# An attention-and-convolution kernel on one core: every product and transpose issued as two halves of 64 stationary columns

## The chip, the core and the metric

The kernel runs on one core of a Trainium2 chip, as one program with one launch. The metric is the time of one execution on the device in microseconds; the figure for a kernel is the median over its runs. All data is fp32.

## What is computed

Eight images of 768 channels by 32 x 32 pixels go through two residual layers. Cut to what matters, the reference is:

```python
# layer 0: attention whose scores come from variances; _gn is a normalisation over 32 groups of channels
qkv = tokens(_gn(x)) @ W_qkv.T                       # 8 x 1024 tokens x (3 x 768); q is not used
var_v, var_k = var(v, per head), var(k, per head)    # one number per token and head (12 heads of 64)
scores = var_v @ var_k.T * scale                     # an outer product, 1024 x 1024 for each head
out = softmax(scores) @ v @ W_proj.T + b_proj
x = x + out
# layer 1: a 1x1 convolution over 768 features and 28 local correlations
f = _gn(x)
corr = 28 sums over channels of shifted, normalised f * f      # a 7x7 neighbourhood, four lines through it
x = x + conv_w @ concat(f, corr) + conv_b
```

## The kernel before

**Products.** The three large products (keys and values, projection, convolution) are each split into 2 x 2 blocks and computed with seven block products instead of eight. A block product is a *unit*: three accumulating matmuls of 128 rows and 128 stationary columns. In `KeysValues.unit` (L592) the stationary operand is the image and the moving operand 384 columns of weights; in `Wide.unit` (L973, projection and convolution) the stationary operand is a weight block and the moving operand 512 tokens. Both hand their list of operand pairs to `Banks.product` (L342), whose `begin` (L345) issues the matmuls at L359 into one of two x banks and two y banks of PSUM; one early case is issued at L605. When a unit is done, VectorE (or ScalarE, for copies of keys and values) takes the bank.

**Attention.** For each image there are six pairs of heads. `Pair.exponentials` (L716) has ScalarE make the exponentials of one token tile for both heads (two passes of 128 x 1024, L721). `Pair.products` (L740) then multiplies them by the values at L746: four matmuls, each of 64 stationary columns, the two heads on columns 0 to 63 and 64 to 127 of the array. Such a step is issued in runs of four (`Attention.run`, L951, `STEPS = 4`). The row sums of the softmax come either from ScalarE (`denominators`, L725) or from accumulated exponentials, summed by a matmul of 32 stationary columns (`sum_up`, L772, L779) or of 64 (`sum_up_last`, L822, L829).

**The rest on TensorE.** `Corr.gram` (L1070, L1083) multiplies shifted windows of the features in matmuls of 64 stationary columns and 133 moving ones, two sides next to each other. `Wide.join` (L986, L990) adds the correlations' part with matmuls of 64 rows and 128 columns, two of them on the upper and the lower half of the rows; `Conv.corr` (L1253, L1260) does it for the last image. Four small things use the whole array: the group means (`Norm.means` L465, `Norm.spreads` L476, one moving column), and the transposes in `to_rows` (L538), `Pair.spread` (L855) and `Corr.scale.to_dram` (L1139).

**Order.** The schedule is by hand: while the program is built, a `Clock` (L77) carries an estimated time forward, units pass it on by `KV_US`, `T_US`, `STEP_US`, `GRAM_US` and `CORR_US` (L52 to L54), and jobs that are due are issued on the way. `work_off` (L1290) puts attention's runs in as soon as its exponentials should be there, and fills the time between with units of key/value products, convolution and grams. So TensorE changes often between products, runs of attention, grams, joins and transposes. Each engine then executes its instructions in the order so written.

Of the kernel before, what the change touches and what calls it, by code (L numbers as in the profile page):

```python
# [6 lines left out]
F32 = mybir.dt.float32  # L7
# [6 lines left out]
P = 128  # L14
# [3 lines left out]
NH, HD = 12, 64  # L18
HP = NH // 2
MT = N // P  # L20
HF = N // 2
# [11 lines left out]
PAD = 99  # L33
# [6 lines left out]
NROW = NA + 2  # L40

HH = NH // 2
# [6 lines left out]
TBLOCKS = 7  # L49
HELD = 12  # L50
TAIL = 14.0
EXP, SUM, STEP_US = 1.07, 1.15, 1.77  # L52
KV_US, T_US, CORR_US = 1.94, 2.6, 1.05
GRAM_US = 1.45  # L54

# [7 lines left out]
FIRST, LAST = (1, 5, 2), (4, 3, 2)  # L65
# [92 lines left out]
def two_layers(ctx, tc, x, wkv, wproj, bproj, wconv, wcorr, bconv, out):  # L158
    nc = tc.nc
# [4 lines left out]
    const = pool("const", 1)  # L164
# [14 lines left out]
    st = pool("st", 1)  # L179
# [9 lines left out]
    vector = Vector(nc.vector, clock)  # L189
    ready = set()  # L190

    def work(shape, name):
        return wk.tile(shape, F32, tag="wk", name=name)
# [136 lines left out]
            return self.tiles.pop(0)  # L330


    class Banks:
        def __init__(self):
            self.count, self.due, self.open, self.free = {"x": 0, "y": 0}, {}, {}, {}
# [9 lines left out]
        def begin(self, g, p, width, pairs, stop=True, between=None):  # L345
            bank = BANK[p]
            of = "x" if bank == "x" else "y"
            if p in FIRST:
                slot = of, self.count[of] % 2
                self.count[of] += 1  # L350
                self.finish(slot)
                clock.pass_time(max(self.free.get(slot, 0.0) - clock.now, 0.0))
                t = (xbank if of == "x" else ybank).tile([P, width], F32, tag=of, name=f"{bank}{self.count[of]}")
                self.open[g, bank] = slot, t
            slot, t = self.open[g, bank]
            self.finish(slot)
            clock.pass_time(max(self.free.get(slot, 0.0) - clock.now, 0.0))
            for k, (lhsT, rhs) in enumerate(pairs):
                nc.tensor.matmul(  # L359
                    t, lhsT=lhsT, rhs=rhs, start=p in FIRST and k == 0, stop=stop and k == len(pairs) - 1,  # L360
                    skip_group_check=True,
                )
                if between and k == 0:
                    between()
            return slot, t
# [12 lines left out]
    ident = const.tile([P, P], F32, name="ident")  # L378
# [3 lines left out]
    for base, sign in ((0, 1), (3, -1)):  # L382
        nc.gpsimd.affine_select(
            out=group, in_=group, compare_op=ALU.is_ge, fill=0.0, base=base,
            pattern=[[-4 * sign, P // 4], [0, 4]], channel_multiplier=sign,
        )
    group_m = group.rearrange("p g r -> p (g r)")
# [5 lines left out]
    neghalf = const.tile([P, 4], F32, name="neghalf")  # L393
    nc.gpsimd.memset(neghalf, -0.5)

    wcorr_sb = const.tile([P, J, P], F32, name="wcorr_sb")
    nc.gpsimd.memset(wcorr_sb, 0.0)
    cs = const.tile([P, 3, HF], F32, name="cs")
# [7 lines left out]
    rows = [dconst.tile([NROW, ROW], F32, name=f"rows{i}") for i in range(2)]  # L406
# [47 lines left out]
    class Norm:  # L454
# [7 lines left out]
        def means(self):  # L462
            name, mv = self.name, self.mv
            pm = small(f"pm{name}")
            nc.tensor.matmul(pm[:, 0:1], lhsT=group_m, rhs=mv[:, 0:1], start=True, stop=True)  # L465
            self.mean = st.tile([P, 1], F32, tag="mean", bufs=2, name=f"mean{name}")
            vector.tensor_copy(self.mean, pm[:, 0:1])
            d = st.tile([P, 1], F32, tag="d", name=f"d{name}")
            vector.tensor_tensor(d, mv[:, 0:1], self.mean, ALU.subtract)
            self.e = st.tile([P, 1], F32, tag="e", bufs=2, name=f"e{name}")  # L470
            vector.scalar_tensor_tensor(self.e, d, d, mv[:, 1:2], ALU.mult, ALU.add)

        def spreads(self):
            name = self.name
            pv = small(f"pv{name}")
            nc.tensor.matmul(pv[:, 0:1], lhsT=group_m, rhs=self.e, start=True, stop=True)  # L476
            ve = st.tile([P, 1], F32, tag="ve", name=f"ve{name}")
            vector.tensor_scalar(ve, pv[:, 0:1], GN_EPS, None, ALU.add)
            self.rstd = st.tile([P, 1], F32, tag="rstd", bufs=2, name=f"rstd{name}")
            nc.gpsimd.tensor_tensor(self.rstd, ve, neghalf[:, 0:1], ALU.pow)  # L480
# [54 lines left out]
    def to_rows(cols, dr, name):  # L535

        pt = small(f"pt{name}")
        nc.tensor.transpose(pt[0 : MT * HH, 0:P], cols.rearrange("p h t -> p (h t)"), ident)  # L538
        rs = work([MT * HH, P], f"rs{name}")
        vector.tensor_copy(rs, pt[0 : MT * HH, 0:P])  # L540
        nc.sync.dma_start(out=dr.rearrange("h (t p) -> (h t) p", p=P), in_=rs)

    class KeysValues:
# [48 lines left out]
        def unit(self, half, d, n, g, p):  # L592
            b = self.b
            if n == 0:
                self.make_sums(half, (2 * d, 2 * d + 1))
            s = self.sums[g]
            a = {1: self.block(g, 0, 0), 2: self.block(g, 0, 1), 4: self.block(g, 1, 1)}
            a.update({5: s[:, 0], 6: s[:, 1], 7: s[:, 2], 3: s[:, 3]})
            w = kv_stream.tiles[b, half, d, p]
            pairs = [(a[p][:, k, :], w[:, k, :]) for k in range(JH)]  # L600
            taken = lambda ps: self.take(half, g, p, ps)
            if p == 2 and not b + half + d:
                ps = other([P, KW], f"z{g}")
                for k, (lhsT, rhs) in enumerate(pairs):
                    nc.tensor.matmul(ps, lhsT=lhsT, rhs=rhs, start=k == 0, stop=k == len(pairs) - 1)  # L605
                later.after(KV_US + 0.1, lambda: taken(ps))
            else:
                banks.product(g, p, KV_US, KW, pairs, taken)
            if p not in [q for _, q in (PAIR if b + half + d else OPENING)[n + 1 :]]:
                kv_stream.done((b, half, d, p))  # L610
            if d == 1 and n == len(PAIR) - 1:
                self.over = half == 1
                later.after(KV_US + 0.5, lambda: later.after_dve(0.0, lambda: self.spread(half)))
# [77 lines left out]
    class Pair:  # L691
# [153 lines left out]
            invert(0)  # L845

        def invert(self):
            self.inv = st.tile([P, 2 * MT], F32, tag="inv", bufs=2, name=f"inv{self.b}_{self.hp}")
            vector.reciprocal(self.inv, self.sums.rearrange("p e t -> p (e t)"))
            later.after_dve(3.5, self.spread)  # L850

        def spread(self):
            b, hp = self.b, self.hp
            pt = small(f"it{b}_{hp}")
            nc.tensor.transpose(pt[0 : 2 * MT, 0:P], self.inv, ident)  # L855
            row = work([2 * MT, P], f"ir{b}_{hp}")
            vector.tensor_copy(row, pt[0 : 2 * MT, 0:P])
            dr = dpool.tile([2 * MT, P], F32, tag="inv", name=f"di{b}_{hp}")
            nc.sync.dma_start(out=dr, in_=row)
            later.after(4.0, lambda: self.load_inverses([dr[e * MT : e * MT + 1, :] for e in range(2)]))  # L860
# [190 lines left out]
    class Corr:  # L1051
# [18 lines left out]
        def gram(self, t):  # L1070
# [32 lines left out]

            later.after(GRAM_US + 0.25, out)

# [16 lines left out]
        def scale(self, hf, dd):  # L1122

            b = self.b
            m = st.tile([P, 4], F32, tag="m", name=f"m{b}_{hf}")
            vector.tensor_scalar(m, dd[:, :, 0], NORM_EPS2, None, ALU.max)
            rn = st.tile([P, 4], F32, tag="rn", name=f"rn{b}_{hf}")
            nc.gpsimd.tensor_tensor(rn, m, neghalf, ALU.pow)

            def columns():  # L1130
                dn = st.tile([P, 4, NROW], F32, tag="dn", name=f"dn{b}_{hf}")
                vector.tensor_copy(dn[:, :, 0], rn)
                for q in range(4):
                    vector.scalar_tensor_tensor(dn[:, q, 1:NROW], dd[:, q, :], rn[:, q : q + 1], mask, ALU.mult, ALU.mult)
                later.after_dve(0.7 if b else 4.0, lambda: to_dram(dn))

            def to_dram(dn):
                pt = small(f"ct{b}_{hf}")
                nc.tensor.transpose(pt[0 : 4 * NROW, 0:P], dn.rearrange("p q r -> p (q r)"), ident)  # L1139
                cr = work([4 * NROW, P], f"cr{b}_{hf}")  # L1140
                vector.tensor_copy(
                    cr.rearrange("k (y s x) -> k y s x", y=4, s=2),
                    pt[0 : 4 * NROW, 0:P].rearrange("k (s y x) -> k y s x", s=2, y=4),
                )
                for q in range(4):
                    at = PAD + hf * HF + q * P
                    nc.sync.dma_start(out=rows[b % 2][:, at : at + P], in_=cr[q * NROW : (q + 1) * NROW, :])
                if hf == 1:
                    later.after(3.0, self.gather)

            later.after_dve(2.5, columns)
# [273 lines left out]
    for b in range(NB + 1):  # L1425
# [6 lines left out]
        if b:  # L1432
# [3 lines left out]
            f, acc = layer1[b - 1] if b > 1 else first_f * 2  # L1436
# [5 lines left out]
            first, start = (0.0, has_f, conv.sums.first), (0.0, (), conv.start)  # L1442
# [69 lines left out]
```

## Time and profile before

| | before |
|---|---|
| median of 3 runs | 2679.1 us (2678.01 to 2680.77) |
| the profiled execution | 2675.76 us |
| its span, first to last instruction | 2674.0 us |
| granted TensorE clock | 0.998 |
| DVE, ACT, POOL busy | 1604.2, 1364.0, 410.8 us |
| DMA, mean | 167 GB/s |

An fp32 matmul appears in the trace as two records (passes), each with a weight load (PEld) of its own; a transpose appears as one. Durations of single matmul records overlap, since matmuls are pipelined: the distance from the start of one to the start of the next is the time that TensorE gives to it. In a line of the timeline, the columns are the start, the length, the engine, the line of code, the operation, out<-in, stationary rows*columns, and the count of records that were merged.

### The profile page before, as it was taken

To read this page: it belongs to the slowest core of one execution; us is meant where nothing else is said; L and a number is where in the kernel's file an instruction comes from. 1 tells how busy PE (TensorE), PEld (TensorE's weight loads), DVE (VectorE), ACT (ScalarE), POOL (GpSimd) and SP (SyncE) were. 2 spreads that over 40 slices of the span, in tenths; PEclk is the share of its full clock that TensorE was granted. 3 is DMA by queue.
4 is the path that set the end of the run, shared out by engine and by line. 5 is a ranking of instruction groups with operands and counts; after the bars stand their busy time and mean duration, and the time that the engine had idled before them with its cause. 6 is when DMAs were issued, how large, how long until landed. Compare 5 with 4: busy or idle time off the path is not lost.

```text
span 2674.0 us, 30536 instructions
## 1 busy us (share of the span) xinstructions
PE 2634.8 (99%) x9831; PEld 1221.7 (46%) x9831; DVE 1604.2 (60%) x4110; ACT 1364.0 (51%) x1841; POOL 410.8 (15%) x442
## 2 busy tenths in 40 slices
PE   7999999999999999999999999999999999999999
PEld 4443454345543355434554345543455434554344
DVE  5758734775446854478534785348753577536864
ACT  1498069711597116970179701797018960189600
POOL 4220030002310033000330003300133001320000
PEclk9999999999999999999999999999999999999999
DMA  7764455455554555536456265562655626545243
GB/s 285 289 226 156 141 187 150 136 185 165 177 171 133 185 156 179 178 114 208 149 172 195 91 212 157 164 206 73 220 169 159 194 83 226 167 136 165 87 125 101
DMA packets 323354, 446.03 MB, mean 167 GB/s; under 512 B 59458, under 2 KB 245170, under 8 KB 323194
## 3 DMA queue, kind: packets, MB, share of 16 engines
q1 hardware_dynamic: 321962, 441.32, 51.6%
q10 hardware_dynamic: 1232, 2.75, 0.3%
q8 instruction: 79, 1.29, 0.2%
q14 instruction: 81, 0.66, 0.1%
HBM read 377.49 MB, written 64.40 MB: 165 GB/s over the span
## 4 chain that ended last, share of the span: by engine, by line
PE 93%; DMA 4%; DVE 2%; issue 0%; ACT 0%; SPq 0%; POOL 0%; DVEq 0%; POOLq 0%; ACTq 0%
PE x L359 36%; PE av L746 24%; PE y L359 17%; PE z L359 9%; PE gr L1083 3%; DMA x<-x1d 1%; PE den L779 1%; PE x L990 1%; PE y L990 1%; PE z L990 1%; DMA vdr<-rsv 0%; DMA x1d<-f 0%; DVE x L152 0%; DVE v L152 0%; PE den L829 0%
## 5 line engine op out<-in xcount | busy, mean ns | idle before, releaser
L721 ACT ACTIVATE ex<-bc,nk 128x1024 f32<-128x1024 f32 x768 | 826.5, 1137 | 432.2 <-DMA bc<-vdr 171.0
L746 PE MATMUL av<-ex,v 128*64 128x512 f32 x3072 | 691.7, 597 | 5.6 <-ACT ex L721 5.6
L731 ACT ACTIVATE junk<-bk,vm 128x1024 bf16<-128x1024 f32 x368 | 420.3, 1142 | 38.3 <-DMA bk<-kdr 32.4
L746 PEld LDWEIGHTS av<-ex,v 128*64 128x64 f32 x3072 | 223.4, 137 | 434.8 <-issue 372.4
L152 DVE TENSOR_TENSOR acc<-acc,ex 128x1024 f32<-128x1024 f32 x300 | 344.7, 1211 | 0.0
L214 ACT COPY kp<-x 128x384 f32<-128x384 f32 x28 | 13.4, 477 | 571.4 <-PE x L359 571.4
L359 PE MATMUL y<-kv,s 128*128 128x384 f32 x744 | 260.6, 491 | 0.2 <-issue 0.2
L359 PE MATMUL x<-kv,xn 128*128 128x384 f32 x756 | 257.2, 489 | 2.8 <-DVE xn L152 1.6
L359 PE MATMUL x<-kv,s 128*128 128x384 f32 x744 | 254.4, 489 | 0.0
L359 PEld LDWEIGHTS x<-kv,xn 128*128 128x128 f32 x756 | 143.5, 191 | 107.2 <-issue 9.1
L359 PEld LDWEIGHTS x<-kv,s 128*128 128x128 f32 x744 | 138.6, 190 | 102.5 <-issue 9.9
L359 PEld LDWEIGHTS y<-kv,s 128*128 128x128 f32 x744 | 137.8, 190 | 94.2 <-issue 7.3
L480 POOL TENSOR_TENSOR rstda<-vea,neghalf 128x1 f32<-128x1 f32 x8 | 4.8, 595 | 1009.5 <-DVE vea L152 1009.5
L1068 POOL TENSOR_TENSOR turn<-f,ones 128x384 f32<-128x384 f32 x112 | 111.6, 1016 | 265.9 <-PE gr L1083 206.5
L359 PE MATMUL x<-v,wt 128*128 128x512 f32 x288 | 130.2, 596 | 0.0
L359 PE MATMUL z<-kv,xn 128*128 128x384 f32 x372 | 126.9, 488 | 0.0
L152 DVE TENSOR_TENSOR v<-y,v 128x128 f32<-128x128 f32 x180 | 41.0, 282 | 138.7 <-PE y L359 138.7
L359 PE MATMUL x<-f,wt 128*128 128x512 f32 x252 | 116.1, 600 | 0.3 <-DVE x L152 0.3
L584 POOL TENSOR_TENSOR s<-xn 128x384 f32<-128x384 f32 x64 | 66.8, 1054 | 287.1 <-PE x L359 193.3
L152 DVE BATCH_NORM_STATS2 vbn<-v 128x6 f32<-128x64 f32 x720 | 101.6, 209 | 0.0
L152 DVE SCALAR_TENSOR_TENSOR x<-x,bconv_sb,x 128x512 f32<-128x512 f32 x63 | 45.8, 746 | 92.6 <-DMA x<-x1d 52.8
L359 PEld LDWEIGHTS z<-kv,xn 128*128 128x128 f32 x372 | 69.9, 190 | 49.2 <-issue 2.3
(191 smaller groups left out, 3012.9 us busy)
## 6 DMA issues: line engine op xcount, KB each, us to landing
kv<-kvs SPq DMA_DIRECT2D x124, 576.0 KB
kv<-in_wkv_dram SPq DMA_DIRECT2D x95, 576.0 KB
bc<-vdr SPq DMA_DIRECT2D x96, 512.0 KB
f<-in_x_dram SPq DMA_DIRECT2D x48, 512.0 KB
bk<-kdr SPq DMA_DIRECT2D x46, 512.0 KB
x1d<-f SPq DMA_DIRECT2D x42, 512.0 KB
x<-x1d SPq DMA_DIRECT2D x42, 512.0 KB
out_dram<-x SPq DMA_DIRECT2D x82, 256.0 KB
```

The source lines that it names most:

```text
L152: return getattr(self.engine, name)(*args, **kw)
L214: nc.scalar.copy(to, at)
L359: nc.tensor.matmul(t, lhsT=lhsT, rhs=rhs, start=p in FIRST and k == 0, stop=stop and k == len(pairs) - 1, skip_group_check=True,)
L480: nc.gpsimd.tensor_tensor(self.rstd, ve, neghalf[:, 0:1], ALU.pow)
L584: nc.gpsimd.tensor_tensor(self.sums[g][:, 0], a[g][2], a[g][3], ALU.add)
L721: nc.scalar.activation(ex, self.bc[e], AF.Exp, scale=self.kv.nk[self.half][:, h, t : t + 1])
L731: nc.scalar.activation(junk, self.bk[e], AF.Exp, scale=self.kv.m2[self.half][:, h, t : t + 1], accum_out=self.sums[:, e, t : t + 1],)
L746: nc.tensor.matmul(self.av[e * HD : (e + 1) * HD, hf, :], lhsT=self.vt[:, t, e, :], rhs=exs[e][:, hf * HF : (hf + 1) * HF], start=t == 0, ...
L779: nc.tensor.matmul(den[at * 32 : (at + 1) * 32, :], lhsT=ones[:, 0:32], rhs=self.acc[e][:, hf * HF : (hf + 1) * HF], start=True, stop=True,)
L990: nc.tensor.matmul(t, lhsT=wcorr_sb[at, i, :], rhs=cs[at, tokens, :], start=False, stop=True, skip_group_check=True)
L1068: nc.gpsimd.tensor_tensor(to[:, :, side], half, windows(ones, ones.ap[0], (0, J), (HW, 4), (1, HW)), ALU.mult)
L1083: nc.tensor.matmul(ps[side * HD : (side + 1) * HD, :n].rearrange("p (y x) -> p y x", x=WIDE), lhsT=block[:, j, side, :], rhs=image[:, 4 * ...
```

## The change

Every matmul of 128 stationary columns at L359, L605, L465 and L476 becomes two of 64 columns, one after the other, with the same moving operand, into the upper and the lower half of the same PSUM tile. The transposes become plain matmuls of 64 (or 48) columns with the identity as the moving operand, without the transpose flag. The one at L855 had 16 columns; its input is now a constant tile of 64 columns of which 16 are filled. The one at L1139 had 80; it is now two of 64 that overlap by 48 columns, and the rows of the last quarter are read from the second. The matmuls of 32 columns (L779) and of 64 rows (L990, L1260) stay. The planner's estimates change.

```diff
-EXP, SUM, STEP_US = 1.07, 1.15, 1.77
-KV_US, T_US, CORR_US = 1.94, 2.6, 1.05
-GRAM_US = 1.45
+EXP, SUM, STEP_US = 1.07, 1.15, 1.73
+KV_US, T_US, CORR_US = 1.93, 2.58, 1.2
+GRAM_US = 1.4
...
+    def halves(out, lhsT, rhs, start=True, stop=True, **kw):
+
+        for at in (slice(0, HD), slice(HD, P)):
+            nc.tensor.matmul(out[at], lhsT=lhsT[:, at], rhs=rhs, start=start, stop=stop, **kw)
+
+    def turned(out, columns):
+        nc.tensor.matmul(out, lhsT=columns, rhs=ident, start=True, stop=True)
+
...
-                nc.tensor.matmul(
-                    t, lhsT=lhsT, rhs=rhs, start=p in FIRST and k == 0, stop=stop and k == len(pairs) - 1,
-                    skip_group_check=True,
+                halves(
+                    t, lhsT, rhs, start=p in FIRST and k == 0, stop=stop and k == len(pairs) - 1, skip_group_check=True
                 )
...
+    invs = [const.tile([P, HD], F32, name=f"invs{n}") for n in range(2)]
+    for t in invs:
+        nc.gpsimd.memset(t, 1.0)
...
-            nc.tensor.matmul(pm[:, 0:1], lhsT=group_m, rhs=mv[:, 0:1], start=True, stop=True)
+            halves(pm[:, 0:1], group_m, mv[:, 0:1])
...
-            nc.tensor.matmul(pv[:, 0:1], lhsT=group_m, rhs=self.e, start=True, stop=True)
+            halves(pv[:, 0:1], group_m, self.e)
...
-        nc.tensor.transpose(pt[0 : MT * HH, 0:P], cols.rearrange("p h t -> p (h t)"), ident)
+        turned(pt[0 : MT * HH, 0:P], cols.rearrange("p h t -> p (h t)"))
...
-                    nc.tensor.matmul(ps, lhsT=lhsT, rhs=rhs, start=k == 0, stop=k == len(pairs) - 1)
+                    halves(ps, lhsT, rhs, start=k == 0, stop=k == len(pairs) - 1)
...
-            self.inv = st.tile([P, 2 * MT], F32, tag="inv", bufs=2, name=f"inv{self.b}_{self.hp}")
-            vector.reciprocal(self.inv, self.sums.rearrange("p e t -> p (e t)"))
+            self.inv = invs[self.hp % 2]
+            vector.reciprocal(self.inv[:, 0 : 2 * MT], self.sums.rearrange("p e t -> p (e t)"))
...
-            nc.tensor.transpose(pt[0 : 2 * MT, 0:P], self.inv, ident)
+            turned(pt[0:HD, 0:P], self.inv)
...
-                nc.tensor.transpose(pt[0 : 4 * NROW, 0:P], dn.rearrange("p q r -> p (q r)"), ident)
-                cr = work([4 * NROW, P], f"cr{b}_{hf}")
+                columns, over = dn.rearrange("p q r -> p (q r)"), 4 * NROW - HD
+                turned(pt[0:HD, 0:P], columns[:, 0:HD])
+                turned(pt[HD:P, 0:P], columns[:, over:])
+                cr = work([P, P], f"cr{b}_{hf}")
...
-                    at = PAD + hf * HF + q * P
-                    nc.sync.dma_start(out=rows[b % 2][:, at : at + P], in_=cr[q * NROW : (q + 1) * NROW, :])
+                    at, row = PAD + hf * HF + q * P, q * NROW + (HD - over) * (q == 3)
+                    nc.sync.dma_start(out=rows[b % 2][:, at : at + P], in_=cr[row : row + NROW, :])
```

More of the change, by code (lines that the diff above doesn't have):

```diff
@@ L1138, in to_dram @@
                 pt = small(f"ct{b}_{hf}")
-                nc.tensor.transpose(pt[0 : 4 * NROW, 0:P], dn.rearrange("p q r -> p (q r)"), ident)
-                cr = work([4 * NROW, P], f"cr{b}_{hf}")
+                columns, over = dn.rearrange("p q r -> p (q r)"), 4 * NROW - HD
+                turned(pt[0:HD, 0:P], columns[:, 0:HD])
+                turned(pt[HD:P, 0:P], columns[:, over:])
+                cr = work([P, P], f"cr{b}_{hf}")
                 vector.tensor_copy(
                     cr.rearrange("k (y s x) -> k y s x", y=4, s=2),
-                    pt[0 : 4 * NROW, 0:P].rearrange("k (s y x) -> k y s x", s=2, y=4),
+                    pt[:, 0:P].rearrange("k (s y x) -> k y s x", s=2, y=4),
                 )
                 for q in range(4):
-                    at = PAD + hf * HF + q * P
-                    nc.sync.dma_start(out=rows[b % 2][:, at : at + P], in_=cr[q * NROW : (q + 1) * NROW, :])
+                    at, row = PAD + hf * HF + q * P, q * NROW + (HD - over) * (q == 3)
+                    nc.sync.dma_start(out=rows[b % 2][:, at : at + P], in_=cr[row : row + NROW, :])
                 if hf == 1:
```

## The prediction, made before the changed kernel ran

> **What bounds the kernel now.** I read the page's busy times first, then its chain, then the stages, then the timeline of TensorE at the places where it changes from one kind of work to another.
>
> ```profile
> span 2674.0 us, 30536 instructions
> ...
> PE 2634.8 (99%) x9831; PEld 1221.7 (46%) x9831; DVE 1604.2 (60%) x4110; ACT 1364.0 (51%) x1841; POOL 410.8 (15%) x442
> ...
> PE 93%; DMA 4%; DVE 2%; issue 0%; ACT 0%; SPq 0%; POOL 0%; DVEq 0%; POOLq 0%; ACTq 0%
> ```
>
> TensorE is busy all the time and 93% of the chain is its own. But a busy PE isn't a PE at its peak: a matmul that waits inside the array counts as busy. So I take the distance from start to start. The timeline of one stage, with key/value products, a transpose, a gram, products, a transpose:
>
> ```profile
> 1008.32 4.03 PE L359 MATMUL x<-kv,xn 128*128 128x384 f32 x12
> 1012.19 2.10 PE L359 MATMUL y<-kv,s 128*128 128x384 f32 x6
> 1014.12 0.27 PE L538 MATMUL ptv<-ident,vm 128*48 128x128 f32 x1
> 1014.32 1.58 PE L1083 MATMUL gr<-f,turn 128*64 128x133 f32 x24
> 1015.84 2.20 PE L359 MATMUL y<-kv,s 128*128 128x384 f32 x6
> 1017.87 0.27 PE L538 MATMUL ptk<-ident,nk 128*48 128x128 f32 x1
> 1017.98 2.42 PE L359 MATMUL x<-kv,s 128*128 128x384 f32 x7
> ```
>
> Twelve passes of a product take 1012.19 - 1008.32 = 3.87 us, 0.3225 each; six take 1.93, the same, though a transpose follows. From a transpose to a product it is 0.11 (1017.87 to 1017.98), to the gram 0.20: 0.09 lost. The gram's 24 records are 12 pairs 0.113 us apart, 1.36, and take 1.52: 0.15 lost. The six passes after it take 2.03, not 1.935: 0.10 lost. About 0.35 us for going into 64 columns and back. Around attention:
>
> ```profile
> 1082.33 2.10 PE L359 MATMUL x<-kv,s 128*128 128x384 f32 x6
> 1084.35 7.09 PE L746 MATMUL av<-ex,v 128*64 128x512 f32 x32
> 1091.37 2.20 PE L359 MATMUL x<-kv,s 128*128 128x384 f32 x6
> 1093.41 0.27 PE L1139 MATMUL ct<-ident,dn 128*80 128x128 f32 x1
> 1093.52 2.10 PE L359 MATMUL y<-kv,s 128*128 128x384 f32 x6
> ```
>
> 2.02 for six passes (0.09 over), 7.02 for 16 pairs of 0.429 (0.15 over), 2.04 for the next six (0.10 over): 0.35 again. So the two shapes run at the same rate (a pair of 64-column passes over 512 takes 0.429 us, as one pass of 128 columns in the projection does) and the change between them costs.
>
> Over the whole trace, all matmul starts split the time thus: 13.8 us before the first; 2552.1 of passes at their steady distance (moving columns / 1.2 per ns + 2.5 ns, which fits 133, 384 and 512); 58.4 at changes of shape; 44.9 of stalls proper; 4.8 after the last start and in remainders. Of the stalls, 31.2 us lie in the first two images; each image from the third to the seventh has under 2.2. The stages say the same:
>
> ```profile
> 0.00:328.00 328.00, 306.03 (x1035) 145.23 (x1036) 235.66 (x650) 159.22 (x210) 67.71 (x80) 1.00 0.64 222
> 328.00:656.00 328.00, 320.07 (x1182) 149.01 (x1181) 193.06 (x446) 169.08 (x221) 54.11 (x56) 0.99 0.51 164
> 656.00:984.00 328.00, 327.47 (x1229) 151.48 (x1228) 193.83 (x505) 171.71 (x234) 51.06 (x54) 1.00 0.52 165
> ```
>
> (length, then busy PE, PEld, DVE, ACT, POOL, clock, DMA): from the third image PE is idle 0.5 us in 328, at full clock.
>
> [...] 93 to 114 ns lost on leaving a shape, none between the two column halves of attention. [...] the 48-column transposes follow products without loss, so they run in the full shape[...]. [...] the trace's first pass after a change loses 104 and 51 (24 with 32 columns), so it is a load that nothing hides.
>
> **The change, part by part.**
> 1. *Changes of shape.* One costs the drain (medians: 93 ns leaving 128x128, 100 leaving 64 columns, 97 leaving 64 rows, 114 leaving 32 columns) plus the first load. Before there are 338, with the transposes counted as full shape: 58.4 us. In the changed program's order of matmuls 116 remain, at joins and 32-column sums: 45 from 64 columns to 64 rows x (100+104) = 9.2; 37 back x (97+51) = 5.5; 17 from 32 to 64 columns x (114+51) = 2.8; 9 from 64 and 8 from the joins to 32 x 0.12 = 2.1. Sum 19.6. **Saved 38.8.** The direct change from 64 columns to 64 rows isn't in the trace; 93 or 100 as its drain moves the sum by 0.3.
> 2. *Halved products.* 4704 passes become pairs. Attention's and gram's pairs give the steady distance of a whole pass, the second half 7 ns after the first, hidden by the next pair. Loads: gram hides two per 0.113 us, a product has 0.3225. Twice the instructions at 4 per 0.3225 us is below gram's 4 per 0.113. **Nothing**; its cover is that overlap, and without it each ns per pass is 4.7 us. No row has the same moving columns in both halves (attention streams two tiles, gram two overlapping windows of one), so this stays the open point; below nothing it can't go, the pass being bound by its columns.
> 3. *Transposes.* 63, each one pass of 109 ns, become two passes: **+6.9**; 16 have two halves, 3.5 more if those don't run side by side.
> 4. *Group means.* 32. A matmul of one column hides no load: 112 ns to the next product and 84 over in that one's first pass, two loads of 128 columns. Half the columns, half of 168: **-2.7** (0 to -5.4).
> 5. *Waits given back.* In the first two images the waits are for loads and ScalarE, and TensorE saves about 8 us there ((58.4-19.6+2.7-6.9)/8 = 4.3 per image); what comes before a wait that ends at a fixed time is lost. I take **+2** (0 to 8). In later images the fourth step of a run starts about 1.0 us after its exponentials end (their buffer is freed by the run's first step), but 0.2, 0.3 and 0.0 in three runs of the second and third pairs, where ScalarE also sums. An earlier TensorE finds these late: **+1** (0 to 8: three runs x eight images x the 0.35 of one excursion).
> 6. *Order.* With the planner's smaller figures some units move one place ahead of a run of attention; the work and the DMAs are the same but for two memsets on POOL (idle 85%) and a copy of 128 rows in place of 80 on DVE, as long by its columns. Nothing: the moved unit's PSUM and weights are those of its neighbour, and if one is late it is part 5.
>
> Sum: -38.8 + 6.9 - 2.7 + 3 = -31.6. Profiled execution 2675.8 - 31.6 = 2644.2 (span about 2642.4). The median shown is 3.3 above that execution; the same 31.6 off 2679.1 gives **2647.5**. Ends: -38.8 + 6.9 - 5.4 = -37.3, or 2641.8; -38.8 + 6.9 + 3.5 + 16 = -12.4, or 2666.7.
>
> **Rivals.** *The gain is waited away* (ScalarE's exponentials and the early loads take both ends of part 5, +16): -34.6 + 16, **2660.5**. For it: slack of 0.0 to 0.3 us; against: ACT is busy 172 of 328 us per image, and its next exponential starts when TensorE frees a buffer, so it moves along. *The halves don't overlap fully* (at L359, both reading the same columns): with two offsets of 6.7 ns per pass, 4704 x 13.4 ns = +63, giving **2710.5** with parts 1, 3, 4 and 5, slower than before; it decides from 31.6 / 4704 = 6.7 ns per pass. Against: 1366 pairs of attention show no such ns. *The loss isn't the shape's* but any change of work's: nothing saved, +6.9 - 2.7, **2683.3**. Against: products to transposes, and x to y to z bank, cost nothing.
>
> **Numbers.** Forecast 81%, waits 13%, offset 4% (half of it near no change, as one offset just cancels the gain), not the shape 2%. About 0.2% (5 us) is what the measurement can tell from no change. Faster 94%, within 2%, slower 4%. The range, 2638 to 2663, takes in the forecast's lower end with the runs' spread and the first rival; above it lie 2 of the rivals and the far end of the waits.
>
> **What would show it.** Right: a product's six passes before and after attention take 1.935 us (2.02 and 2.04 now), 16 attention pairs 6.87; a pair of a product's halves every 0.3225 or 0.429; 116 changes worth 20 us; images 328 us apart now, then 324. Wrong: pairs at a larger distance, second halves starting late, stalls before attention's fourth steps, or losses where the shape doesn't change.

## The result, and the profile after

| | before | changed |
|---|---|---|
| median | 2679.24 us (2678.01 to 2680.77, 4 runs) | 2657.34 us (2655.61 to 2658.48, 4 runs) |
| ratio | | 0.9917, 95% interval 0.9900 to 0.9935 |
| profiled execution | 2675.76 us, span 2674.0 | 2655.61 us, span 2653.9 |

Faster by 21.9 us, where 31.6 were forecast (2647.5): inside the range, 9.8 us short. The page of the changed kernel, with the lines that answer to those of before:

```profile
span 2653.9 us, 40302 instructions
...
PE 2602.3 (98%) x14694; PEld 1307.0 (49%) x14694; DVE 1605.4 (60%) x4110; ACT 1368.4 (52%) x1841; POOL 414.3 (16%) x444
...
PE 91%; DMA 4%; DVE 2%; ACT 1%; issue 1%; SPq 1%; POOL 0%; DVEq 0%; POOLq 0%; ACTq 0%
```

There are half as many matmul records again, in less time, and the chain has 1% each in ScalarE, SP's queue and issue that it did not have. The same stage as before in TensorE's timeline (products, a transpose, a gram, products, a transpose):

```profile
1010.19 2.10 PE L336 MATMUL y<-kv,s 128*64 128x384 f32 x12
1012.12 0.27 PE L339 MATMUL ptv<-ident,vm 128*48 128x128 f32 x1
1012.13 0.33 PE L1093 MATMUL gr<-f,turn 128*64 128x133 f32 x1
1012.23 0.27 PE L339 MATMUL ptv<-ident,vm 128*48 128x128 f32 x1
1012.29 1.46 PE L1093 MATMUL gr<-f,turn 128*64 128x133 f32 x22
1013.54 0.49 PE L336 MATMUL y<-kv,s 128*64 128x384 f32 x1
1013.59 0.28 PE L1093 MATMUL gr<-f,turn 128*64 128x133 f32 x1
1013.70 2.10 PE L336 MATMUL y<-kv,s 128*64 128x384 f32 x11
1015.64 0.27 PE L339 MATMUL ptk<-ident,nk 128*48 128x128 f32 x1
```

Six pairs of halves take 1.93 us (1010.19 to 1012.12): a pair costs what a pass of 128 columns did. The gram begins 0.01 us after the transpose, beside it, and ends with no loss: from 1013.70, the product's second record, to 1015.64 it is 1.94, where the product took 2.03. The 0.35 us of the excursion into 64 columns and back are gone, and the transpose's second pass is added: from the transpose to the next one it is 3.52 us (1012.12 to 1015.64), where it was 3.75 (1014.12 to 1017.87). Around a group mean, from the mean's first record to the product behind it, it is now 0.08 us:

```profile
1257.74 0.23 PE L336 MATMUL pma<-mva,group 128*64 128x1 f32 x4
1257.82 2.77 PE L336 MATMUL x<-v,wt 128*64 128x512 f32 x12
1260.43 0.23 PE L336 MATMUL pva<-ea,group 128*64 128x1 f32 x4
```

and was 0.14 before, when 128 columns were loaded for it and not 64 (its weight-load records last 205 ns there on average, and 146 now):

```profile
1263.38 0.28 PE L465 MATMUL pma<-mva,group 128*128 128x1 f32 x2
1263.52 2.82 PE L359 MATMUL x<-v,wt 128*128 128x512 f32 x6
```

The stages (length, then busy PE, PEld, DVE, ACT, POOL, clock, DMA) show where it went less well:

```profile
0.00:328.00 328.00, 304.81 (x1663) 162.04 (x1665) 234.64 (x651) 159.74 (x210) 70.95 (x83) 0.99 0.65 223
328.00:656.00 328.00, 314.02 (x1726) 148.22 (x1724) 192.95 (x443) 168.72 (x220) 52.85 (x56) 0.97 0.51 162
656.00:984.00 328.00, 326.56 (x1860) 166.88 (x1858) 194.92 (x509) 173.33 (x236) 51.32 (x54) 1.00 0.52 167
```

In the second stage TensorE is busy 314.0 us; before it was 320.1. From the third stage on it does the work of 328 us in 324, but it stands idle 6 us longer in the second. The start of each image's attention, less the same start in the kernel before, shows it in times (us; "end" is the last instruction; the last three rows are experiments below):

```
image              1     2     3     4     5     6      7      8      end
changed          -0.5  -0.7  +2.8  -0.8  -4.8  -9.1  -13.2  -16.3  -20.1
e1 old order      0.0  -2.1  -5.5  -9.1 -13.1 -17.3  -20.7  -24.2  -27.0
e2 order only    +1.0  +2.5 +10.8 +11.3 +10.7 +10.0   +9.5   +8.7   +7.8
e12 first two    +0.8  -2.5  -2.9  -6.4 -11.2 -15.4  -18.0  -21.2  -24.8
```

From the fourth image to the eighth the changed kernel gains 15.5 us in four images, 3.9 each (forecast 4.3). Up to the third image's attention it has gained nothing and lost 2.8. Each row is one execution against one of the kernel before (2675.76 us, under all four that make its median). A difference of a few microseconds that arises in the first two images can be that of the execution: e6 below, as fast as the kernel before in its medians, stands at +5.2 at the third image and +5.3 at the end. So what the order costs is taken from medians.

### The profile page after: what moved, and what is told of

The parts are those of the page before. It is cut to its first block, busy times and chain, and to the rows that moved or that the text cites. A ratio compares the mean times of both kernels' runs of the same rounds, so it can differ in the third digit from the quotient of the medians.

```text
span 2653.9 us, 40302 instructions
## 1 busy us (share of the span) xinstructions
PE 2602.3 (98%) x14694; PEld 1307.0 (49%) x14694; DVE 1605.4 (60%) x4110; ACT 1368.4 (52%) x1841; POOL 414.3 (16%) x444
## 4 chain that ended last, share of the span: by engine, by line
PE 91%; DMA 4%; DVE 2%; ACT 1%; issue 1%; SPq 1%; POOL 0%; DVEq 0%; POOLq 0%; ACTq 0%
PE x L336 36%; PE av L756 23%; PE y L336 18%; PE z L336 9%; PE gr L1093 3%; DMA x<-x1d 1%; PE den L789 1%; ACT ex L731 1%; PE x L1000 1%; PE y L1000 1%; DMA kv<-kvs 1%; PE z L1000 0%; DMA x1d<-f 0%; DVE x L152 0%; DMA xn<-in_x_dram 0%
## 5 line engine op out<-in xcount | busy, mean ns | idle before, releaser
L756 PEld LDWEIGHTS av<-ex,v 128*64 128x64 f32 x3072 | 322.1, 138 | 345.3 <-issue 206.2
L741 ACT ACTIVATE junk<-bk,vm 128x1024 bf16<-128x1024 f32 x368 | 420.5, 1143 | 31.6 <-DMA bk<-kdr 25.5
L336 PE MATMUL y<-kv,s 128*64 128x384 f32 x1488 | 269.9, 487 | 0.0
L336 PE MATMUL x<-kv,xn 128*64 128x384 f32 x1512 | 265.7, 488 | 1.6 <-DVE xn L152 1.6
L336 PE MATMUL x<-kv,s 128*64 128x384 f32 x1488 | 259.3, 486 | 0.0
L336 PEld LDWEIGHTS x<-kv,xn 128*64 128x64 f32 x1512 | 144.0, 138 | 103.8 <-issue 82.7
L336 PEld LDWEIGHTS x<-kv,s 128*64 128x64 f32 x1488 | 144.2, 137 | 92.1 <-issue 68.8
L336 PEld LDWEIGHTS y<-kv,s 128*64 128x64 f32 x1488 | 140.0, 137 | 87.1 <-issue 68.6
L336 PE MATMUL z<-kv,xn 128*64 128x384 f32 x768 | 135.6, 486 | 0.0
L336 PE MATMUL x<-v,wt 128*64 128x512 f32 x576 | 131.1, 594 | 0.0
L336 PE MATMUL x<-f,wt 128*64 128x512 f32 x504 | 119.5, 593 | 0.0
```

Source lines behind the costliest of these rows:

```text
L336: nc.tensor.matmul(out[at], lhsT=lhsT[:, at], rhs=rhs, start=start, stop=stop, **kw)
L741: nc.scalar.activation(junk, self.bk[e], AF.Exp, scale=self.kv.m2[self.half][:, h, t : t + 1], accum_out=self.sums[:, e, t : t + 1],)
L756: nc.tensor.matmul(self.av[e * HD : (e + 1) * HD, hf, :], lhsT=self.vt[:, t, e, :], rhs=exs[e][:, hf * HF : (hf + 1) * HF], start=t == 0, ...
```

## The experiments

**First: the order, and the price of a change of shape.** The theory (1): what is missing was lost because the planner's smaller estimates put the work of the first two images into a worse order. The rival: a faster TensorE just meets waits that end at fixed times.

`e1_old_order`:

```diff
-EXP, SUM, STEP_US = 1.07, 1.15, 1.73
-KV_US, T_US, CORR_US = 1.93, 2.58, 1.2
-GRAM_US = 1.4
+EXP, SUM, STEP_US = 1.07, 1.15, 1.77
+KV_US, T_US, CORR_US = 1.94, 2.6, 1.05
+GRAM_US = 1.45
```

> The changed kernel with the planner's old estimates (1.77, 1.94, 2.6, 1.05, 1.45), so that every engine gets its work in the order of the kernel before; the halved matmuls stay. Theory 1, the order: what was missing from the gain (2657.3 measured, 2647.5 forecast) was lost in the second image because the new order puts the correlations' small loads behind big ones on SP's queue. Then image 1's attention is no longer behind, and the time is 2645 to 2650 us. Rival, the waits: the first two images wait for loads and for ScalarE that end at fixed times whatever the order; then it stays at 2655 to 2660 us.

Measured: 2650.64 us (2647.81 to 2652.53), ratio 0.9894 (0.9879 to 0.9909); 6.7 under the changed kernel, and its slowest run is faster than the changed kernel's fastest. The order is worth that much; the remaining 3.1 us to the forecast are not the order's.

`e2_new_order_only`: the kernel before with the five new estimates (the edit above turned round, on the old code).

> The kernel before with the planner's new estimates alone; products and transposes keep 128 columns. Its order has 322 changes of shape in place of 338, worth -2.7 us. Theory 1, the order: the second image is held up as in the changed kernel, by 8 to 12 us, and the time is 2684 to 2689 us. Rival, the waits: the order is innocent, and the time is 2675 to 2679 us.

Measured: 2685.03 us, ratio 1.0022 (1.0013 to 1.0032): slower, though it changes shape less often. Here every matmul is as before, so that the sum can be made exactly as for the kernel before: 2552.1 us of passes in both, changes of shape 55.8 (58.4 before, 2.6 less; 2.7 expected), stalls (all that is above the steady distance and not at a change of shape) 55.3 (44.9). The 10.4 us of added stalls less 2.6 are the 7.8 by which its span grew; by its median it is 5.0 slower, so the order costs 7.6 us here. Of the added stalls 9.5 us lie before 656 us, most of that in the second stage of its trace:

```profile
0.00:328.00 328.00, 304.12 (x1031) 144.94 (x1032) 233.08 (x649) 159.74 (x210) 68.87 (x79) 1.00 0.64 220
328.00:656.00 328.00, 314.87 (x1159) 143.23 (x1158) 190.15 (x421) 168.91 (x220) 49.31 (x52) 0.98 0.50 160
```

`e3_real_transposes`:

```diff
-        turned(pt[0 : MT * HH, 0:P], cols.rearrange("p h t -> p (h t)"))
+        nc.tensor.transpose(pt[0 : MT * HH, 0:P], cols.rearrange("p h t -> p (h t)"), ident)
...
-            turned(pt[0:HD, 0:P], self.inv)
+            nc.tensor.transpose(pt[0 : 2 * MT, 0:P], self.inv[:, 0 : 2 * MT], ident)
...
-                turned(pt[0:HD, 0:P], columns[:, 0:HD])
-                turned(pt[HD:P, 0:P], columns[:, over:])
+                nc.tensor.transpose(pt[0 : 4 * NROW, 0:P], columns, ident)
```

> The changed kernel with its 63 transposes as real transposes again (full shape, one pass). By the prices of the forecast [...] 242 changes in place of 116 cost 16.6 us more, and one pass less for each transpose saves 6.9: 9.7 slower than the changed kernel, 2667 us (2664 to 2671). Rival, the loss isn't the shape's: only the passes count, 6.9 faster, 2650 us.

Measured: 2667.69 us (2666.58 to 2670.58), 10.4 over the changed kernel; 9.7 were expected. Its timeline has both kinds of border side by side:

```profile
1083.19 4.04 PE L336 MATMUL x<-kv,s 128*64 128x384 f32 x24
1087.06 7.04 PE L756 MATMUL av<-ex,v 128*64 128x512 f32 x32
1094.03 0.31 PE L1150 MATMUL ct<-ident,dn 128*80 128x128 f32 x1
1094.27 2.16 PE L336 MATMUL y<-kv,s 128*64 128x384 f32 x12
1096.25 4.04 PE L336 MATMUL x<-kv,xn 128*64 128x384 f32 x24
```

Products to attention, both of 64 columns: 12 pairs in 3.87 us, no loss. Attention to a transpose in full shape: 16 pairs in 6.97, 0.10 over 6.87. The transpose takes 0.24 where its pass is 0.11, and the product after it 1.98, 0.05 over. So the loss goes with the shape, not with a change of work, and the third rival of the prediction falls. The product's halves, which stream the same columns, hide as attention's do, so the second falls too.

`e4_keys_values_halved`:

```diff
-                halves(
+                (halves if width == KW else nc.tensor.matmul)(
                     t, lhsT, rhs, start=p in FIRST and k == 0, stop=stop and k == len(pairs) - 1, skip_group_check=True
                 )
```

> The changed kernel with only the key/value products halved (384 moving columns); projection and convolution (512) keep 128 columns, all else as in the changed kernel. By the prices of the forecast 273 changes of shape in place of 116 cost 29.0 us more: 2686 us (2681 to 2691). Rival, the loss isn't the shape's: 2657 us as the changed kernel. If halving the 512-column products itself costs or saves something, it shows as the difference from 2686.

Measured: 2679.10 us, 21.8 over the changed kernel and the same as before (ratio 1.0002). Expected were 29.0. Its profiled execution (2681.25 us, the slowest of its 12) is 25.6 over the changed kernel's (2655.61, the fastest of its four). Image by image it loses 2.8 to 4.1 us from the second on (29.0 over eight images is 3.6 each), but nothing in the first, which has waits (0.7 behind at the second image's attention, after 1.3 at the first's). The count of changes is right in the images where TensorE has next to no waits, and too large in the first.

**Second: where in the order?** In the second image the fourth pair of heads waits for its rows. Two views of SP's queue, the changed kernel:

```profile
462.26 0.36 SPq L551 DMA_DIRECT2D vdr<-rsv  x1
466.69 1.74 SPq L720 DMA_DIRECT2D bc<-vdr  x4
```

and before:

```profile
457.74 0.32 SPq L541 DMA_DIRECT2D vdr<-rsv  x1
466.05 1.75 SPq L710 DMA_DIRECT2D bc<-vdr  x4
```

The store is issued 4.5 us later, although the transpose that it needs now starts at 449.88 and not at 453.35. In between stand eleven small loads of the first image's correlations (`gather`), which in the new order come behind loads of 512 and 576 KB. So the refined theory 1a: SP's queue. The rival 1b: ScalarE's order, in which three row sums (`junk`) stood ahead of the fourth pair's first exponentials (`ex`) and now one does. Before:

```profile
459.93 1.16 ACT L731 ACTIVATE junk<-bk,vm 128x1024 bf16<-128x1024 f32 x1
...
461.21 1.15 ACT L731 ACTIVATE junk<-bk,vm 128x1024 bf16<-128x1024 f32 x1
...
462.49 1.15 ACT L731 ACTIVATE junk<-bk,vm 128x1024 bf16<-128x1024 f32 x1
...
470.10 1.15 ACT L721 ACTIVATE ex<-bc,nk 128x1024 f32<-128x1024 f32 x1 [6.38 <-DMA bc<-vdr]
```

and changed:

```profile
460.00 1.16 ACT L741 ACTIVATE junk<-bk,vm 128x1024 bf16<-128x1024 f32 x1
...
470.69 4.47 ACT L731 ACTIVATE ex<-bc,nk 128x1024 f32<-128x1024 f32 x4 [9.44 <-DMA bc<-vdr]
```

`e5_gathers_off_sp`:

```diff
+            queue = nc.sync if self.b else nc.gpsimd
...
-            nc.sync.dma_start(out=u[0:NA, :], in_=r[2:NROW, PAD : PAD + N])
+            queue.dma_start(out=u[0:NA, :], in_=r[2:NROW, PAD : PAD + N])
```

(and so for the other loads in `gather`).

> The changed kernel with the eleven loads of the first image's correlations (gather) issued from POOL's queue in place of SP's; order and estimates as in the changed kernel. Theory 1a, SP's queue: in the second image these loads wait behind big ones and hold back the store of the values' row (vdr) and the loads of bc behind it, so ScalarE starts the fourth pair late. Then the store is issued before 456 us in place of 462.3, and 4 to 7 us of the 6.7 that the new order costs come back: 2650 to 2653 us. Rival 1b, ScalarE's own order of exponentials and row sums (also changed by the estimates) makes the loss: 2655 to 2659 us.

Measured: 2657.39 us, unchanged. Theory 1a falls. The store did go out early, and it did not help:

```profile
451.71 0.36 SPq L551 DMA_DIRECT2D vdr<-rsv  x1
463.98 1.75 SPq L720 DMA_DIRECT2D bc<-vdr  x4
```

That is 10.6 us earlier than in the changed kernel, but the loads of the row that it stores started only 2.7 us earlier: SP's queue issued nothing in the 11.9 us between (452.07 to 463.98). The 2 us that the trace shows won by then are gone again before the last image.

`e6_gathers_late_before`, the kernel before:

```diff
-                    later.after(3.0, self.gather)
+                    later.after(3.0 if b else 7.0, self.gather)
```

> The kernel before with one estimate changed: the first image's gather is issued 7.0 us after the correlations' rows, not 3.0, so that its loads come behind three big loads of x on SP's queue; every other order stays. Theory 1a, SP's queue: slower than before by 3 to 7 us, 2683 to 2687 us, with the loss in the second image's attention. Rival 1b, ScalarE's order: no change, 2678 to 2682 us.

Measured: 2679.53 us, ratio 1.0007 (0.9998 to 1.0015): no change that can be measured. Its trace has the store at 466.99 us and the loads at 470.33, 4.3 us later than before, and the median doesn't move. It says the same from the other side.

`e7_transpose_earlier`:

```diff
-                later.after_dve(0.7 if b else 4.0, lambda: to_dram(dn))
+                later.after_dve(0.7 if b else 2.5, lambda: to_dram(dn))
```

> The changed kernel with the first image's correlation transpose due 2.5 us after its columns, not 4.0, so that its four stores go ahead of the inverse's store on SP's queue as in the kernel before, and the gathers behind two big loads instead of four. Theory 1a: a part of the 6.7 comes back, 2651 to 2656 us. Rival 1b: 2655 to 2659 us.

Measured: 2656.59 us, unchanged. The store went out at 457.16 us and the loads at 463.30, 3.4 us before the changed kernel's: again not SP's queue. (The edit also moved some other work of the second image on TensorE, ScalarE and SP, so it is a less clean test than e5.)

`e8_old_order_alternate`:

```diff
-        turned(pt[0 : MT * HH, 0:P], cols.rearrange("p h t -> p (h t)"))
+        at = HD if name[0] == "k" else 0
+        turned(pt[at : at + MT * HH, 0:P], cols.rearrange("p h t -> p (h t)"))
...
-            turned(pt[0:HD, 0:P], self.inv)
+            at = HD * (1 - hp % 2)
+            turned(pt[at : at + HD, 0:P], self.inv)
```

> The changed kernel in the old order (2650.6 us), with the single transposes put on the two column halves in turn: keys and every second inverse on columns 64 to 127. A single one holds one half for two passes of 0.109 us while the other goes on; if two of them on different halves lie in the same stretch between changes of shape, one is hidden. At most half of 47 x 0.218 = 5.1 us: 2645.5 to 2650; expected about 2648. If a half can't run ahead of the other at all: 2650.6, unchanged.

Measured: 2651.05 us (2649.49 to 2653.82), against 2650.64 without it: no gain that can be measured.

**Third: ScalarE's order and the planner's estimate.**

`e9_sums_first`:

```diff
             def job():
+                if (pair.b, pair.hp, t) == (1, HP // 2, 0):
+                    for n, (us, may, sums) in enumerate(clock.rows[1][:2]):
+                        sums()
+                        clock.rows[1][n] = us, may, lambda: None
                 pair.exponentials(t)
```

> The changed kernel with ScalarE's order at one place as in the kernel before: in the second image, two more row sums of the third pair of heads go ahead of the fourth pair's first exponentials (which wait for loads), and the order on TensorE and SP stays. Theory 1b, ScalarE's order: the two sums (2 x 1.28 us) no longer stand between exponentials that TensorE waits for, and about 2.6 us come back: 2654 to 2656 us. If the loss lies elsewhere (TensorE's own order, or the loads alone): 2657 us, unchanged.

`e10_sums_first_gathers_off` has the edits of e5 and e9.

> Both at once: the two sums ahead, and the first image's gathers on POOL's queue, which brought the fourth pair's exponentials of the second image 2.5 us earlier in its trace. If the new order's 6.7 us are these two waits in the second image, most of it comes back: 2651 to 2653.5 us. If a part is TensorE's own order (one product less left to fill in before the fourth pair), it stays above: 2654 to 2657 us.

`e11_later_estimate`:

```diff
+            if (self.b, self.hp, kind) == (1, HP // 2, "c"):
+                self.rows_at[kind, e] += 4.5
```

> The changed kernel with one estimate made true: in the second image the planner takes the fourth pair's rows (bc) to be there 4.5 us later than it did. Then it puts three more sums ahead and the order of TensorE's work around the fourth pair follows. If the loss is the planner's error at this place, 2651 to 2654 us; the loads still come late (SP), so not all comes back. If the loss is spread over many places: 2655 to 2658 us.

Measured: 2653.70, 2654.03 and 2653.64 us; ratios 0.9899 (0.9883 to 0.9914), 0.9906 (0.9892 to 0.9920) and 0.9904 (0.9890 to 0.9918). Each is some 3.5 us under the changed kernel by its median, about what theory 1b expected of e9 (2654 to 2656). The intervals of their ratios overlap the changed kernel's 0.9900 to 0.9935, but so does that of e1. Run by run, all four of e9 and 10 of the 13 of the three kernels lie under all 12 of the changed kernel, e5 and e7 (2655.61 to 2659.35). So by the medians ScalarE's order at this one place (e9), or the planner's estimate that sets it (e11), makes about half of the order's 6.7 us. Where the time comes back is less clear: in e10's and e11's traces the third image's attention starts 2.6 and 2.8 us earlier than in the changed kernel, but in e9's it does not (3.0 us later than before), and there the fourth pair's loads came 1.6 us later. Taking the gathers away as well (e10) adds nothing.

**Fourth: which images?** `e12_old_order_first_two`, with the old estimates at the head of the file:

```diff
     for b in range(NB + 1):
+        if b == 2:
+            globals().update(STEP_US=1.73, KV_US=1.93, T_US=2.58, CORR_US=1.2, GRAM_US=1.4)
         rest, attention, ots, beside = [], None, None, []
```

> The changed kernel with the planner's old estimates while it plans the first two images and the new ones from the third on: its order is that of the old-order run (2650.6 us) up to there, and that of the changed kernel (2657.3) after it. If the new order's loss lies in the first two images: 2648 to 2652 us, with 13 or more of the changed kernel's loss there gone by the third image's attention in the trace. If it lies in the later images: 2655 to 2658. If in both: between.

Measured: 2650.24 us (2649.27 to 2652.60), ratio 0.9891 (0.9875 to 0.9908): as e1. The 12 runs of e1, e8 and e12, which share the old order in the first two images, lie between 2647.81 and 2653.82 us, all under the 12 of the new order named above. The loss by the order lies in the first two images, all of it within the measurement. (The expectation's "13 or more" for the trace has no counterpart; in the table e12 stands 5.7 us ahead of the changed kernel at the third image and 4.6 at the end.) e12 and e1, equal within their spread, are the fastest kernels here, faster than both that were compared.

What waits there, in the second image's attention from 465 to 520 us (total us, times, longest): before, changed, and e1:

```profile
PE av L746 <- ACT ex L721: 4.0, 3, 2.8
```

```profile
PE av L756 <- ACT ex L731: 8.4, 2, 4.5
```

```profile
PE av L756 <- ACT ex L731: 6.1, 3, 3.1
```

In e1, in the order of before, attention waits 2.1 us longer than before; that would be the rival's part. But single traces differ by as much: e12, with e1's order up to here, waits 4.3 us, and e6, with nearly the order of before, 4.9. So the rival's part isn't shown. The order's part is: the traces in the new order (also e2 7.8, e5 7.6) wait longer than all in the old (4.0 to 6.1), and e11, with the later estimate at this place, waits 4.9. Two smaller waits of the first two images also go with the new order: 2.6 us for the accumulated exponentials before a sum (L789; 1.2 before, 1.4 in e1, 2.6 in e2 and e5) and 0.9 for a product's operand, which waits for none before. The wait for the turned features before a gram does not (4.7 changed, 4.1 in e5; 3.9 before, 4.1 in e1).

These waits don't add up to 6.7 us, and a part of the rest can be the clock (0.97 in the changed kernel's second stage above, 0.99 before). In the first two images every trace has one to four stretches of 3.4 or 6.8 us with a granted clock of 0.5, each across or just behind an idle time of TensorE of 1.9 us or more. The changed kernel in the second image, a stretch (columns as in the stages above) and TensorE's timeline:

```profile
470.50:477.20 6.70, 5.31 (x12) 2.55 (x14) 1.23 (x1) 6.42 (x7) 0.00 (x0) 0.50 1.01 382
```

```profile
471.89 8.62 PE L756 MATMUL av<-ex,v 128*64 128x512 f32 x24 [4.47 <-ACT ex L731]
484.41 3.52 PE L756 MATMUL av<-ex,v 128*64 128x512 f32 x7 [3.90 <-ACT ex L731]
```

In such a stretch attention's pairs start 0.853 us apart and not 0.429, so behind the wait of 4.47 us 12 pairs take 8.62 us, where 12 times 0.429 is 5.15. Half of TensorE's busy time in these stretches is an estimate of what they cost: in the first two images 3.3 us before, 8.1 in the changed kernel, 1.5 in e1, 4.6 in e12, 5.7 in e2, 4.9 in e5. In these traces every idle time of 3.3 us or more after the first matmul has such a stretch, and some of 2.6 to 3.1 us have none, as e1's two in the second image (3.12 and 2.79). So the longer waits of the new order are followed by slow passes too. How much of the 6.7 us that makes is not settled: e5 has 3.2 us less of it than the changed kernel and is no faster.

## Why the prediction was right, and where it was off

- **Bound: right.** TensorE bound the kernel, and from the third image on a saving on it is a saving in time (3.9 of 4.3 us per image).
- **Part 1, changes of shape: right.** 116 are left, and the trace of the changed kernel puts 19.7 us on them (19.6 forecast); e2, e3 and e4 each moved their number. In e2's sum the price held within 0.1 us, in e3's time within 0.7; in e4 the time fell short by 7 us in the medians and 3 in the traces, in the traces all in the first image. The drain and the first load of the prediction are shown as lost time: 93 to 114 ns on leaving a shape, then 104, 51 and 24 in the first pass with 128, 64 and 32 stationary columns. In the trace of before a weight-load record lasts 190, 137 and 108 ns with 128, 64 and 32 columns, 53 and 29 apart, where the losses in the first pass are 53 and 27 apart. What the array does while it changes shape is not shown.
- **Part 2, halved products: right.** 0.3225 us per pair, and no cost for streaming the same columns twice.
- **Part 3, transposes: right as part of e3's sum,** 10.4 against 9.7. The gram above runs beside a transpose, but the second pass isn't hidden: on the transpose's half two passes of it, 12 of the gram and six of the product are 0.22 + 1.36 + 1.94 = 3.52 us, which is what passed. That a transpose must be a plain matmul to stay in the shape of 64 columns was the author's assumption: in e3's trace one of 16 columns (at 1081.00 us) and one of 80 (at 1094.03), both with the flag, lose 0.10 us before them and 0.05 after; with the flag and 64 columns none was run.
- **Part 4, group means: right,** a little small: from a mean's last record to the product 52 ns in place of 112, and the pass after it 30 ns over in place of 84; 0.114 us for each of 32, 3.6 us in place of 2.7. (112 and 84 are 196 ns; the prediction halved 168 of them.)
- **Part 5, waits given back: too small.** 3 us were forecast, 16 was the bound. In e1, which has the old order, the span fell 26.9 us where parts 1, 3 and 4 give 34.6: 7.7 us went to waits. By the medians (2680.04 to 2650.64) it is 5.2. By the account of matmul starts, less exact here because the halves are out of step, the stalls grew by 8.3 us, 4.1 of them before 656 us. For the others the fourth steps of attention were the forecast's place, and in the third pairs of the later images a fourth step's first matmul does start 0.5 us before its second exponential ends in e1, where before the two fell together. But it is not shown that this costs the time: in e12, whose order from the third image on leaves these steps 0.5 us or more of slack, an image gains no more than in e1 (3.7 us in both, third to eighth). That passes behind a long wait can run at half clock, as shown above, was in no part.
- **Part 6, order: wrong.** It said "Nothing", with the words that a unit that is late is part 5. (The copy that it calls as long by its columns takes 287 ns with 80 rows and 292 with 128. That an engine runs its work in the order written shows in the trace of before: by the tiles that they write, 1472 instructions of ScalarE, all but the reads of its accumulator and a table load, and all 4110 of VectorE stand as in the program.) The order costs 6.7 us (e1 against the changed kernel) and 7.6 in e2 (5.0 by the median, with 2.6 saved on shapes). The prediction looked at what each moved unit needs; it did not look at ScalarE's sums, which move with the same estimates (about half of the cost: e9, e11). That less work is then left to fill TensorE's wait for the fourth pair's rows is likely and was not tried alone.
- **Rivals.** The first, "the gain is waited away" (2660.5), was nearest in its time, but for another reason: the waits without the new order take 5 to 8 us, not 16, and the order the rest. The offset and "not the shape's" fell.
- **The range.** That the time fell inside it is in part luck: the room above 2647.5 was made for waits, and 6.7 of the 9.8 us that filled it came from the order, which was put at nothing.

What stays open: which of the moved items in the first two images make the other half of the 6.7 us. SP's queue does not (e5, e6, e7), and two row sums make about half by the medians (e9). TensorE's own order there, with one convolution product less left between the third and the fourth pair, was not tried alone, nor was the clock apart from the waits.

## What to carry to other kernels

Measure matmuls from start to start: "99% busy" hid 58 us lost at 338 changes of array shape, 93 to 114 ns on leaving a shape and 24 to 104 in the first pass after it. Here 222 changes fewer brought some 29 us in the old order (e1), 0.13 us for each one taken out, with the second pass of every transpose paid. When a change also moves a hand-made schedule's estimates, test the two apart: the new estimates cost a quarter of the gain here, in the two images that have waits, and none in the others. A count of savings held to about a tenth in the images where the bounding engine has no waits (3.9 of 4.3 us); where it has, take a part of it off at once, and look at the granted clock behind each long wait (0.5 for 3.4 or 6.8 us here).

## What the runs showed that was not expected

The two column halves don't stay in step. A transpose on one half is overtaken by the gram or the product that follows it: the record of the gram at 1012.13 us stands between the two passes of the transpose at 1012.12 and 1012.23, and after it the halves of the products run half a pass apart (starts 0.16 us from each other, pairs still 0.3225 apart). Moving every second transpose to the other half (e8) brought nothing all the same.

A small store of 24 KB, issued at 451.7 us in e5, let the loads that need it start only at 464.0, 12.3 us later; issued at 462.3 in the changed kernel, 4.4 us later. On this queue, with loads of 512 and 576 KB ahead, the time of issue said little about the time of landing.
